# First two layers' last three tiles one by one, fewer products in the attention among slices, and small last groups in the de-slice

## The chip, the cores and the metric

One core of one Trainium2 chip runs one kernel launch. The metric is device time in microseconds (us); the median of several runs is the figure compared. The engines that appear below are TensorE (PE, with its weight loads as PEld), VectorE (DVE), ScalarE (ACT), GpSimd (POOL) and SyncE (SP), each with its own instruction queue; SP, ACT and POOL also issue DMAs (SPq, ACTq, POOLq).

## The reference

A graph of 6250 nodes with 256 features and 106,250 directed edges (loops among them) passes four blocks, each with a normalisation ahead of it and added to its input. Cut to what matters here:

```python
# block 1: two rounds of "sum over neighbours", each followed by an MLP (GIN)
h = (1 + eps1) * x + segment_sum(x[src], dst)          # layer 1
h = relu(h @ W1a + b1a); h = relu(h @ W1b + b1b)       # 256 -> 512 -> 512
h = (1 + eps2) * h + segment_sum(h[src], dst)          # layer 2
out = relu(h @ W2a + b2a) @ W2b + b2b                  # 512 -> 512 -> 256
# block 2: attention among 64 slices in each of 8 heads
fx = x @ W_fx + b_fx;  x_mid = x @ W_x + b_x
sw = softmax((x_mid @ W_slice + b_slice) / temp)       # node -> slice weights
token = einsum("nc,ng->gc", fx, sw) / (sw.sum(nodes) + 1e-5)   # per head
q, k, v = token @ W_q, token @ W_k, token @ W_v        # 64 x 64 each
o = softmax(q @ k.T * 64 ** -0.5) @ v
out = (sw @ o, heads side by side) @ W_out + b_out     # the de-slice
# block 3: a GCN layer (gather, sum, batch norm, relu) = layer 3
# block 4: a mixture of 8 experts, top 2, 256 -> 512 -> 256
```

The kernel applies W2a before the second sum over neighbours (the sum is linear), so that layer 1 writes h @ W2a as the table that layer 2 gathers from.

## The kernel before

**Tiles and chunks.** The nodes are cut into 49 tiles of 128 (tile 48 has 106). The sums over neighbours are made tile by tile: 831 chunks of 128 edges, 17 for a tile and 11 for tile 48. For each chunk POOL gathers 128 rows of a table in DRAM (L152); DVE builds a 128 x 128 matrix of zeros and ones that says which edge goes to which node; PE multiplies (L173, three bf16 products that together carry the fp32 value) and collects in PSUM. The class `Sums` does this, with a ring of gather buffers (10 deep in layer 1, 32 in layer 2). A table must be whole before the first gather of its layer: T2 (written at L698 in layer 1) for layer 2, T3 (written at L978 by ACT's DMA queue) for layer 3. Edges beyond the planned chunks are handled by `rest`, a loop that runs zero times on these inputs.

**Layers 1 and 2.** Tiles are grouped; when a group's sums are complete, a generator (`gin1` L652 to L700 for layer 1, `gin2` L784 to L865 for layer 2) gives the rest of its work in pieces. `staggered` (L354) puts these pieces between the chunks of the *next* group, so that PE works on one group's products while POOL gathers for the next. In `gin1` a group's pieces are the transposes (L349), W1a (L673), W1b (L681), and for each tile W2a (L688), the split into three bf16 parts (L691 to L697) and the writes of S2 and T2. In `gin2` they are the transposes of the sum (L804), W2b (L811), the normalisation, the transposes of the normalised tile (L349), the slice logits (L832), their softmax (L834 to L844), the token products (L852, added up in `tok`), and the transposed weights (L861), kept in SW for the de-slice. `begin` (L776) loads S2 for a group ahead of its sums.

`groups(4, 5)` in layer 1 gives fours, then [40-43], [44,45], [46,47], [48]. `groups(2)` in layer 2 gives pairs, then [46,47], [48]. `groups(4)` in the de-slice gives fours, then [44-47], [48].

**The attention core** (L870 to L952) runs once, after tile 48's token products: reciprocals of the slice sums (L889), the mean tokens and their transposes (L894 to L903), the token product with W_fx and the bias b_fx (L919, L920; for each of 8 heads two products of 128 rows and one of a single row), q and k (L926), v (L928), the logits (L930), their softmax (L934 to L940), the transposes (L941), o (L943), and W_out applied per head (L950), which gives M, 512 x 256. PE, DVE and ACT follow the order that the tile scheduler works out from the program; its PSUM buffers are those that layer 2 has freed.

**The de-slice** (L955 to L978) goes over the tiles once more: it reloads X1 and SW (three buffers of `swT`), multiplies SW with M (L968), adds, normalises for layer 3 (L329), splits into three bf16 parts (ACT L334, L337; DVE L335, L338), and writes T3. Layer 3 and the experts follow with an order written out by hand, which the change doesn't touch.

Of the kernel before, what the change touches and what calls it, by code (L numbers as in the profile page):

```python
# [9 lines left out]
F32 = mybir.dt.float32  # L10
BF16 = mybir.dt.bfloat16
I32 = mybir.dt.int32
AF = mybir.ActivationFunctionType
# [4 lines left out]
P = 128  # L18
# [3 lines left out]
def gin_transolver_gcn_moe(ctx: ExitStack, tc: tile.TileContext, a: dict, out: bass.AP):  # L22
# [38 lines left out]
    def groups(j, small=0):  # L61

        n = max(0, NT - small) // j * j
        out = [list(range(t, min(t + j, NT))) for t in range(0, n if small else NT, j)]
        while small and n < NT:
            m = 2 if NT - n > 2 else 1
            out.append(list(range(n, n + m)))
            n += m
        return out
# [281 lines left out]
            nc.scalar.activation(dest[:, k0:k0 + len(ks), :J * P],  # L351
                                 p[:, :len(ks) * J * P].rearrange("p (k n) -> p k n", k=len(ks)), AF.Copy)

    def staggered(gs, sums, finish, pieces):  # L354

        work = iter(())
        for ts in gs:
            nxt = finish(ts)
            for j, t in enumerate(ts):
                sums(t, lambda: next(work, None), (j + 1) * pieces // len(ts) - j * pieces // len(ts))  # L360
                next(nxt)
            for _ in work:
                pass
            work = nxt
        for _ in work:
            pass


# [386 lines left out]
    with tc.tile_pool(name="attn", bufs=1) as ap_:  # L755
# [3 lines left out]
        with tc.tile_pool(name="g2w", bufs=1) as wp:  # L759
# [5 lines left out]
            with tc.tile_pool(name="bn", bufs=1) as bnw, \  # L765
# [4 lines left out]

                needs = third_needs(bnw, ps)

                pairs = groups(2)
                s_of = {}

                def begin(ts):  # L776
                    s = w.tile([P, 2, HID], F32, name="s", bufs=3)
                    nc.sync.dma_start(s[:, :len(ts), :], tiles_of(S2, ts))
                    for j, t in enumerate(ts):
                        s_of[t] = s[:, j, :]  # L780

                begin(pairs[0])

                def gin2(ts):  # L784
                    J = len(ts)
                    if ts[0] in (4, 10):
                        next(needs, None)
                    xt = w.tile([P, 2, D], F32, name="xt")
                    if ts is not pairs[-1]:
                        begin(pairs[ts[0] // 2 + 1])  # L790
                    s = [s_of[t] for t in ts]
                    for j, t in enumerate(ts):
                        r = rows_of(t)
# [70 lines left out]
                            yield  # L864
                    nc.sync.dma_start(tiles_of(SW, ts), swT[:, :J, :])  # L865

                staggered(pairs, Sums(T2, msgs, 32, hots, ps, halves_added(lambda t: s_of[t], HID)), gin2, 11)


        res = ctx.enter_context(tc.tile_pool(name="res", bufs=1, side="right"))  # L870
# [2 lines left out]
        bw = back.enter_context(tc.tile_pool(name="desl", bufs=2))  # L873
        with tc.tile_pool(name="core", bufs=1) as w, \
                tc.tile_pool(name="core_ps", bufs=2, space=PSUM) as ps:
            Wfx = weights(w, a["L0_ffn_W_fx"], "Wfx")
            bfx = row(w, a["L0_ffn_b_fx"], H * C, "bfx")
            Wo = w.tile([C, H, D], F32, name="Wo")
            nc.sync.dma_start(Wo, a["L0_ffn_W_out"].rearrange("(h c) d -> c h d", c=C))
            wq = {}  # L880
            for n in ("W_q", "W_k", "W_v"):
                wq[n] = w.tile([C, C], F32, name=n)
                nc.sync.dma_start(wq[n], a["L0_ffn_" + n])

            def pst(name):
                return ps.tile([P, 512], F32, name=name, tag="mm")

            rec = w.tile([P, 2, KG], F32, name="rec")
            nc.vector.tensor_scalar(rec[:, 0, :], tok[:, :, D], 1e-5, None, op0=OP.add)  # L889
            nc.vector.reciprocal(rec[:, 0, :], rec[:, 0, :])  # L890
            nc.vector.tensor_mul(rec[:, 1, :], rec[:, 0, :], tok[:, :, D])
            prow = pst("prow")
            for m in range(KG):
                nc.vector.tensor_scalar(tok[:, m, :D], tok[:, m, :D], rec[:, 0, m:m + 1], None, op0=OP.mult)  # L894
                nc.tensor.transpose(prow[0:1, m * P:(m + 1) * P], rec[:, 1, m:m + 1], ident)
            nrow = w.tile([1, HG], F32, name="nrow")
            nc.vector.tensor_copy(nrow, prow[0:1, :HG])
            meanT = w.tile([P, KD, HG], F32, name="meanT")
            for k in range(KD):
                p = pst("pm")  # L900
                for m in range(KG):
                    nc.tensor.transpose(p[:, m * P:(m + 1) * P], tok[:, m, k * P:(k + 1) * P], ident)
                nc.vector.tensor_copy(meanT[:, k, :], p[:, :HG])  # L903

            def taken(p, name):
                t = w.tile([C, HG], F32, name=name)
                nc.vector.tensor_copy(t, p[:C, :HG])
                return t

            def per_head(name, f):  # L910
                p = pst("p" + name)
                for h in range(H):
                    s = slice(h * G, (h + 1) * G)
                    f(p[:C, s], s, h)
                return p

            def token(o, s, h):
                for k in range(KD):
                    nc.tensor.matmul(o, Wfx[:, k, s], meanT[:, k, s], start=(k == 0), stop=False)  # L919
                nc.tensor.matmul(o, bfx[:, s], nrow[:, s], start=False, stop=True)  # L920

            tokT = taken(per_head("tok", token), "tokT")
            qk = {}
            for n in ("W_q", "W_k"):
                p = pst("p" + n)
                nc.tensor.matmul(p[:C, :HG], wq[n], tokT, start=True, stop=True)  # L926
                qk[n] = taken(p, n + "T")
            v = taken(per_head("v", lambda o, s, h: nc.tensor.matmul(  # L928
                o, tokT[:, s], wq["W_v"], start=True, stop=True)), "v")
            p = per_head("l", lambda o, s, h: nc.tensor.matmul(  # L930
                o, qk["W_q"][:, s], qk["W_k"][:, s], start=True, stop=True))
            p3 = p[:C, :HG].rearrange("p (h g) -> p h g", g=G)
            mx = w.tile([C, 2, H], F32, name="mx")
            nc.vector.tensor_reduce(mx[:, 0, :], p3, axis=AX.X, op=OP.max)  # L934
            at = w.tile([C, H, G], F32, name="at")
            nc.vector.tensor_tensor(at, p3, mx[:, 0, :, None].to_broadcast([C, H, G]), op=OP.subtract)
            nc.scalar.activation(at, at, AF.Exp, scale=float(C) ** -0.5)
            nc.vector.tensor_reduce(mx[:, 1, :], at, axis=AX.X, op=OP.add)
            nc.vector.reciprocal(mx[:, 1, :], mx[:, 1, :])
            nc.vector.tensor_tensor(at, at, mx[:, 1, :, None].to_broadcast([C, H, G]), op=OP.mult)  # L940
            atT = taken(per_head("at", lambda o, s, h: nc.tensor.transpose(  # L941
                o, at[:, h, :], ident[:C, :C])), "atT")
            oT = taken(per_head("o", lambda o, s, h: nc.tensor.matmul(  # L943
                o, v[:, s], atT[:, s], start=True, stop=True)), "oT")

            for m in range(KG):
                p = pst("pM")
                for r in range(P // G):
                    h = m * (P // G) + r
                    nc.tensor.matmul(p[r * G:(r + 1) * G, :D], oT[:, h * G:(h + 1) * G], Wo[:, h, :],  # L950
                                     start=True, stop=True)
                nc.vector.tensor_copy(M[:, m, :], p[:, :D])  # L952


        with back, tc.tile_pool(name="desl_ps", bufs=2, space=PSUM) as ps:  # L955
            w = bw
            for ts in groups(4):
                J = len(ts)
                x1 = xr[:, ts[0]:ts[-1] + 1, :]
                nc.sync.dma_start(x1, block(X1, ts))  # L960
                swT = w.tile([P, 4, HG], F32, name="swT", bufs=3)
                nc.sync.dma_start(swT[:, :J, :], tiles_of(SW, ts))
                for j0 in range(0, J, 2):
                    js = range(j0, min(j0 + 2, J))
                    p = ps.tile([P, 2, D], F32, name="po", tag="mm", bufs=4)
                    for j in js:
                        for m in range(KG):
                            nc.tensor.matmul(p[:, j - j0, :], swT[:, j, m * P:(m + 1) * P], M[:, m, :],  # L968
                                             start=(m == 0), stop=(m == KG - 1))
                    nc.vector.tensor_add(x1[:, j0:js[-1] + 1, :], x1[:, j0:js[-1] + 1, :], p[:, :len(js), :])  # L970

                hs = w.tile([P, 4, D], F32, name="hs")
                layer_norm(w, x1, J, [hs[:, j, :] for j in range(J)], dinv[:, ts[0]:ts[-1] + 1],
                           ln3[:, :, ts[0]:ts[-1] + 1])
                hr = w.tile([P, 4, 3, D], BF16, name="hr")
                for _ in split(hr[:, :J], hs[:, :J, :], hs[:, :J, :], nc.vector.tensor_tensor):
                    pass
                nc.scalar.dma_start(block(T3, ts), hr[:, :J].rearrange("p j s f -> p j (s f)"))  # L978
# [406 lines left out]
```

## Time and profile before

| What | us |
|---|---|
| Six runs: median (lowest to highest) | 4011.18 (4002.73 to 4014.57) |
| Profiled execution: its own time / its span | 4004.99 / 4003.3 |
| First gather of layer 2 begins (from the span's start) | 1233.84 |
| Last gather of layer 2 issued | 2354.73 |
| Last token sum of layer 2 done, the core begins | 2396.60 |
| M done, the de-slice's products begin | 2427.09 |
| First gather of layer 3 begins | 2531.56 |

The span runs from the first to the last instruction. PE is busy for 74% of it and POOL for 65%, but the page's shares are means over stages with different limits; a stage's own window tells what limits it. A granted clock of 1.00 means that PE ran at full speed, 0.50 at half; a row's DMA share is the mean busy share of the 16 DMA engines. In a timeline row the bracket gives how long the engine stood idle before, and what ended that.

### The profile page before, as it was taken

What the parts mean: (1) busy time and instruction counts of PE and PEld (TensorE: products, weight loads), DVE (VectorE), ACT (ScalarE), POOL (GpSimd) and SP (SyncE); (2) the same over time, 40 slices, a digit from 0 to 9 for tenths busy, and PEclk for the clock granted to TensorE, in tenths of its full rate; (3) what the DMA queues carried; (4) which work ended last, traced back from release to release, by engine and by line L of the source; (5) the groups of instructions that cost most, each with busy time, mean ns of one, the idle gap of its engine ahead of it and who ended that gap; (6) DMA issues with size and microseconds to landing.
All of it is one profiled execution on the core that took longest, in us unless ns stands there. A gap on an engine that the chain in (4) does not pass through costs nothing. (4 is left out here: it accounts for less than half of the span.)

```text
span 4003.3 us, 44258 instructions
## 1 busy us (share of the span) xinstructions
PE 2976.3 (74%) x14455; PEld 1904.4 (48%) x14456; DVE 1525.9 (38%) x3910; ACT 783.3 (20%) x1474; POOL 2589.1 (65%) x2723
## 2 busy tenths in 40 slices
PE   2577787777886888888888879566777777777774
PEld 1344344444453444444444447344555566566654
DVE  7122222222322444444444446343334444433342
ACT  5011111111121111111111124111222222222221
POOL 3766677777764766676777730576766666666664
PEclk6588888898899999999999998667777887878887
DMA  6777777777777999999999966557777777778877
GB/s 197 241 265 257 271 247 252 242 251 224 238 239 267 323 323 318 319 327 328 325 333 326 321 233 224 154 167 251 261 261 251 239 250 244 257 262 302 287 262 231
DMA packets 352699, 1058.23 MB, mean 264 GB/s; under 512 B 60061, under 2 KB 147975, under 8 KB 337104
## 3 DMA queue, kind: packets, MB, share of 16 engines
q0 software_dynamic: 183024, 679.31, 52.2%
q1 hardware_dynamic: 162960, 366.42, 25.1%
q10 hardware_dynamic: 6480, 9.63, 0.7%
q8 instruction: 115, 1.88, 0.2%
q14 instruction: 120, 0.98, 0.1%
HBM read 881.24 MB, written 173.88 MB: 264 GB/s over the span
## 5 line engine op out<-in xcount | busy, mean ns | idle before, releaser
L152 POOL DMA_INDIRECT msg<-T,srcT x2493 | 2365.6, 949 | 1226.6 <-issue 615.8
L173 PE MATMUL pa<-msg,hot 128*128 128x257 bf16 (+2 forms) x7479 | 1514.3, 336 | 866.0 <-DMA msg<-T,srcT 819.8
L173 PEld LDWEIGHTS <-hot 128*128 128x128 bf16 x7479 | 782.0, 105 | 1533.7 <-issue 1147.8
L194 DVE SCALAR_TENSOR_TENSOR hot<-dstT,node 128x1152 bf16<-128x1152 f32 (+2 forms) x297 | 373.4, 1260 | 23.8 <-PE pa L173 23.8
L1208 PE MATMUL ph<-xdT,wb 128*128 128x128 f32 x1792 | 250.9, 290 | 45.3 <-DMA wb<-WB 24.9
L1208 PEld LDWEIGHTS ph<-xdT,wb 128*128 128x128 f32 x1792 | 226.8, 200 | 67.7 <-issue 21.6
L642 DVE TENSOR_TENSOR dinv<-dinv,pa 128x1 f32<-128x1 f32 x145 | 22.3, 154 | 591.9 <-PE pa L173 590.7
L1215 PE MATMUL py<-wb,hT 128*128 128x256 f32 x896 | 222.2, 392 | 0.1
L1210 ACT ACTIVATE hT<-ph,wb 128x128 f32<-128x128 f32 x448 | 163.8, 367 | 236.9 <-PE ph L1208 221.5
L681 PE MATMUL p<-h1T,W1b 128*128 128x512 f32 (+2 forms) x448 | 196.1, 586 | 0.0
L688 PE MATMUL p<-W2a,h2T 128*128 128x512 f32 x392 | 192.3, 637 | 0.0
L1215 PEld LDWEIGHTS py<-wb,hT 128*128 128x128 f32 x896 | 165.4, 195 | 22.5 <-ACT hT L1210 2.8
L998 DVE TENSOR_TENSOR s<-s,pa 64x256 f32<-64x256 f32 x96 | 40.2, 419 | 327.3 <-PE pa L173 325.2
L152 POOL DMA_INDIRECT g<-XD,place x98 | 95.6, 976 | 70.1 <-DMA XD<-yd 26.6
L351 ACT ACTIVATE sT<-pt 128x512 f32<-128x512 f32 (+1 forms) x25 | 14.7, 589 | 633.8 <-PE pt L349 633.8
L1111 POOL DMA_INDIRECT XD<-xn,place x98 | 97.4, 994 | 51.1 <-issue 18.0
L235 DVE TENSOR_TENSOR s<-s,pa 128x512 f32<-128x512 f32 x49 | 33.5, 683 | 251.1 <-PE pa L173 251.1
L236 DVE TENSOR_TENSOR s<-s,pa 64x512 f32<-64x512 f32 x48 | 33.2, 691 | 236.8 <-PE pa L173 236.8
L681 PEld LDWEIGHTS p<-h1T,W1b 128*128 128x128 f32 x448 | 86.6, 209 | 75.8 <-issue 73.2
L673 PE MATMUL p<-h0T,W1a 128*128 128x512 f32 (+2 forms) x224 | 120.4, 670 | 1.1 <-ACT h0T L351 0.5
L852 PE MATMUL ptok<-xn,sw 128*128 128x257 f32 (+1 forms) x392 | 103.0, 397 | 18.2 <-DVE sw L844 17.8
L688 PEld LDWEIGHTS p<-W2a,h2T 128*128 128x128 f32 x392 | 77.4, 208 | 81.4 <-issue 80.4
(303 smaller groups left out, 3069.8 us busy)
## 6 DMA issues: line engine op xcount, KB each, us to landing
wb<-WB SPq DMA_DIRECT2D x112, 1154.0 KB
XD<-zeros SPq DMA_DIRECT2D x102, 512.0 KB
msg<-T,srcT POOLq DMA_INDIRECT x2493
T<-tp SPq DMA_DIRECT2D x49, 384.0 KB
xd<-XD SPq DMA_DIRECT2D x112, 128.0 KB
XD<-yd SPq DMA_DIRECT2D x112, 128.0 KB
S<-s SPq DMA_DIRECT2D x49, 256.0 KB
s<-S SPq DMA_DIRECT2D x24, 512.0 KB
```

The lines of the kernel that those rows point to most:

```text
L152: return nc.gpsimd.indirect_dma_start(out=msg, out_offset=None, in_=table, in_offset=bass.IndirectOffsetOnAxis(ap=ix, axis=0))
L173: nc.tensor.matmul(pa[:, :n], hot, msg[:, s * F:s * F + n], start=(start and s == 2), stop=(stop and s == 1))
L194: nc.vector.scalar_tensor_tensor(hot[:, :n, :], dstT[:, c0:c0 + n, None].to_broadcast([P, n, P]), float(k * HALF), node2[:, k % 2, None, : ...
L673: nc.tensor.matmul(p[:, :T], W1a[:, k, m * P:(m + 1) * P], h0T[:, k, :T], start=(k == 0), stop=(k == KD - 1))
L681: nc.tensor.matmul(p[:, :T], W1b[:, k, m * P:(m + 1) * P], h1T[:, k, :T], start=(k == 0), stop=(k == KH - 1))
L688: nc.tensor.matmul(p, h2T[:, k, j * P:(j + 1) * P], W2a[:, k, :], start=(k == 0), stop=(k == KH - 1))
L852: nc.tensor.matmul(p[:, :D + 1], sws[j][:r, m * P:(m + 1) * P], xn[:r, j, :], start=(j == 0), stop=(j == J - 1))
L998: nc.vector.tensor_add(s3s[t][rows], s3s[t][rows], pa[rows, :D])
L1111: ins = nc.gpsimd.indirect_dma_start(out=XD[i], out_offset=bass.IndirectOffsetOnAxis(ap=place[:r, t, c:c + 1], axis=0), in_=xn[:r, j, :], ...
L1208: nc.tensor.matmul(p[:, :P], W1[:, k, m * P:(m + 1) * P], xdT[:, k, :P], start=(k == 0), stop=(k == KD - 1))
L1210: nc.scalar.activation(hT[:, m, :], p[:, :P], AF.Relu, bias=b1[:, m:m + 1])
L1215: nc.tensor.matmul(p[:, :D], hT[:, m, :], W2[:, m, :], start=(m == 0), stop=(m == KH - 1))
```

## The change

- `groups` gives pairs only while more than four tiles are left, so that `groups(4, 5)` ends in [44,45], [46], [47], [48]. Layer 2 uses `groups(2, 3)`, which ends in ..., [44,45], [46], [47], [48], and the de-slice `groups(4, 5)`.
- `staggered` gets `aside`: in layer 2 only 5 of tile 47's 11 pieces go between tile 48's chunks; then two pieces of 48, and then 47's other pieces and 48's in turn. `begin` loads S2 two groups ahead.
- In the core, two products of weights alone are formed first: kq from W_q and W_k, and vo from W_v and W_out for each head (three 64 x 64 transposes, one 64 x 64 product, four 64 x 512 products). The logits then come from tokT and one product kq by tokT; v is formed with vo (64 x 256 for each head) and M from the attention and v, so that q, the product o and its copy go. b_fx is added by one product of 8 rows with a mask `of_head` instead of eight of one row. PSUM tiles have four buffers instead of two, and some copies move from DVE to ACT.

```diff
@@ groups
-            m = 2 if NT - n > 2 else 1
+            m = 2 if NT - n > 4 else 1
@@ staggered
-    def staggered(gs, sums, finish, pieces):
+    def staggered(gs, sums, finish, pieces, aside=False):
         work = iter(())
         for ts in gs:
             nxt = finish(ts)
+            n = pieces // 2 if aside and ts is gs[-1] else pieces
             for j, t in enumerate(ts):
-                sums(t, lambda: next(work, None), (j + 1) * pieces // len(ts) - j * pieces // len(ts))
+                sums(t, lambda: next(work, None), (j + 1) * n // len(ts) - j * n // len(ts))
                 next(nxt)
+            if n < pieces:
+                break
             for _ in work:
                 pass
             work = nxt
+        for _ in range(2):
+            next(nxt, None)
         for _ in work:
+            next(nxt, None)
+        for _ in nxt:
             pass
@@ layer 2
-                pairs = groups(2)
+                pairs = groups(2, 3)
...
                 begin(pairs[0])
+                begin(pairs[1])
...
-                    if ts is not pairs[-1]:
-                        begin(pairs[ts[0] // 2 + 1])
+                    if ts not in pairs[-2:]:
+                        begin(pairs[pairs.index(ts) + 2])
...
-                staggered(pairs, Sums(...), gin2, 11)
+                staggered(pairs, Sums(...), gin2, 11, True)
@@ core
             def pst(name):
-                return ps.tile([P, 512], F32, name=name, tag="mm")
+                return ps.tile([P, 512], F32, name=name, tag="mm", bufs=4)
...
+            of_head = w.tile([H, H, G], F32, name="of_head")
+            nc.vector.memset(of_head, 1.0)
+            for op, base in ((OP.is_ge, 0), (OP.is_gt, 1)):
+                nc.gpsimd.affine_select(out=of_head, in_=of_head, ...)
+            p = pst("pwT")
+            for i in range(3):
+                nc.tensor.transpose(p[:C, i * C:(i + 1) * C], wq[:, i, :], ident[:C, :C])
+            wT = w.tile([C, 3, C], F32, name="wT")
+            nc.scalar.activation(wT, p[:C, :3 * C].rearrange("p (i c) -> p i c", i=3), AF.Copy)
+            p = pst("pkq")
+            nc.tensor.matmul(p[:C, :C], wT[:, 1, :], wT[:, 0, :], start=True, stop=True)
+            kq = w.tile([C, C], F32, name="kq")
+            nc.scalar.activation(kq, p[:C, :C], AF.Copy)
+            vo = w.tile([C, H, D], F32, name="vo")
+            for h in range(0, H, 2):
+                p = pst("pvo")
+                nc.tensor.matmul(p[:C, :2 * D], wT[:, 2, :], Wo[:, h:h + 2, :], start=True, stop=True)
+                nc.scalar.activation(vo[:, h:h + 2, :], p[:C, :2 * D].rearrange("p (h d) -> p h d", h=2), AF.Copy)
...
-                for k in range(KD):
-                    nc.tensor.matmul(o, Wfx[:, k, s], meanT[:, k, s], start=(k == 0), stop=False)
-                nc.tensor.matmul(o, bfx[:, s], nrow[:, s], start=False, stop=True)
+            p = pst("ptok")
+            nc.tensor.matmul(p[:C, :HG], bfx, nrow, start=True, stop=False)
+            for h in range(H):
+                o = slice(h * G, (h + 1) * G)
+                for k in range(KD):
+                    nc.tensor.matmul(p[:C, o], Wfx[:, k, o], meanT[:, k, o], start=False,
+                                     stop=(h == H - 1 and k == KD - 1))
...
-            for n in ("W_q", "W_k"):
-                p = pst("p" + n)
-                nc.tensor.matmul(p[:C, :HG], wq[n], tokT, start=True, stop=True)
-                qk[n] = taken(p, n + "T")
-            v = taken(per_head("v", lambda o, s, h: nc.tensor.matmul(
-                o, tokT[:, s], wq["W_v"], start=True, stop=True)), "v")
-            p = per_head("l", lambda o, s, h: nc.tensor.matmul(
-                o, qk["W_q"][:, s], qk["W_k"][:, s], start=True, stop=True))
+            p = pst("pk")
+            nc.tensor.matmul(p[:C, :HG], kq, tokT, start=True, stop=True)
+            kT = taken(p, "kT")
+            p = pst("pl")
+            for h in range(H):
+                o = slice(h * G, (h + 1) * G)
+                nc.tensor.matmul(p[:C, o], tokT[:, o], kT[:, o], start=True, stop=True)
...
+            v = w.tile([C, H, D], F32, name="v")
+            for h in range(0, H, 2):
+                p = pst("pv")
+                for i in range(2):
+                    nc.tensor.matmul(p[:C, i * D:(i + 1) * D], tokT[:, (h + i) * G:(h + i + 1) * G], vo[:, h + i, :],
+                                     start=True, stop=True)
+                nc.scalar.activation(v[:, h:h + 2, :], p[:C, :2 * D].rearrange("p (h d) -> p h d", h=2), AF.Copy)
...
-            oT = taken(per_head("o", lambda o, s, h: nc.tensor.matmul(
-                o, v[:, s], atT[:, s], start=True, stop=True)), "oT")
...
-                    nc.tensor.matmul(p[r * G:(r + 1) * G, :D], oT[:, h * G:(h + 1) * G], Wo[:, h, :],
+                    nc.tensor.matmul(p[r * G:(r + 1) * G, :D], atT[:, h * G:(h + 1) * G], v[:, h, :],
@@ de-slice
-            for ts in groups(4):
+            for ts in groups(4, 5):
```

## The prediction

> **What bounds the kernel now.** I read, in this order, the page's table of groups, then PE's waits and the windows around the four stretches that the diff touches, then the timeline of each. The page first (engine sums, and the two groups that fill the layers; the last columns are busy time, mean of one, and idle time before with what ended it):
>
> ```profile
> PE 2976.3 (74%) x14455; PEld 1904.4 (48%) x14456; DVE 1525.9 (38%) x3910; ACT 783.3 (20%) x1474; POOL 2589.1 (65%) x2723
> L152 POOL DMA_INDIRECT msg<-T,srcT x2493 | 2365.6, 949 | 1226.6 <-issue 615.8
> L173 PE MATMUL pa<-msg,hot 128*128 128x257 bf16 (+2 forms) x7479 | 1514.3, 336 | 866.0 <-DMA msg<-T,srcT 819.8
> ```
>
> The three layers are paced by POOL's gathers. No gather of a layer can start before the previous layer's table is whole, so between layers POOL stands still, and those two gaps are what this change can shorten:
>
> ```profile
> 1233.84 0.94 POOL L152 DMA_INDIRECT msg<-T,srcT  x1 [39.30 <-issue]
> 2531.56 0.94 POOL L152 DMA_INDIRECT msg<-T,srcT  x1 [175.89 <-issue]
> ```
>
> The bracket is POOL's idle time. Gap 1 (39.30 us) is the end of layer 1. Gap 2 (175.89 us) is the end of layer 2, the attention core, and the de-slice. In the windows (length, then busy time and instructions of PE, PEld, DVE, ACT, POOL; granted clock; DMA) I see four regimes:
>
> ```profile
> 1149.36:1212.98 63.62, 56.46 (x272) 40.10 (x270) 15.01 (x29) 13.55 (x26) 33.09 (x35) 0.92 0.62 203
> 1212.98:1233.84 20.86, 10.08 (x59) 7.20 (x58) 7.83 (x14) 6.44 (x15) 0.00 (x1) 0.89 0.71 204
> 2359.00:2396.60 37.60, 22.28 (x69) 13.64 (x68) 16.79 (x34) 9.32 (x14) 0.00 (x0) 0.82 0.42 137
> 2404.00:2428.00 24.00, 17.24 (x94) 11.08 (x93) 8.72 (x15) 1.91 (x2) 0.00 (x0) 0.50 0.79 254
> 2432.00:2513.70 81.70, 81.70 (x379) 71.62 (x377) 64.70 (x169) 46.10 (x76) 0.00 (x0) 1.00 0.60 206
> PE pa L173 <- DMA msg<-T,srcT: 7.1, 6, 2.1
> ```
>
> Row 1 is tiles 46 to 48 of layer 1 on PE, row 2 tile 48's own multilayer part, row 3 the same end in layer 2, row 4 most of the core at half clock, row 5 the de-slice, PE without a hole. The last line is PE's wait list in row 1's window: 7.1 us in six waits, all on gathers.
>
> **Layer 1's end.** Moved: the products of [44,45] into tile 46's sums, of 46 into 47's, of 47 into 48's; before, [44,45] was spread over 46 and 47, and [46,47] all fell on 48, where PE was busy 20.88 of the 20.88 us from 1192.10 to 1212.98. A single tile costs 2.58 (L673) + 3.79 (L681) + 3.60 (L688) + 0.44 (L349) = 10.4 us on PE; the pair's rows give 4.96, 3.62 + 1.89 + 1.89 = 7.40, and 7.20, so two singles cost 0.4 us more than a pair. A chunk is 20.7 us / 45 = 0.46 us on PE (the 135 L173 matmuls of row 1's window); POOL issued 35 gathers in the 44.24 us to 1193.60, 1.26 us each. So tile 46 asks PE for about 20 + 17 x 0.46 = 28 us against 17 x 1.26 = 21.5 us of gathers, and PE falls 6 us behind; tile 47 asks for 10.4 + 7.8 = 18.2 against 21.5, which the lag covers; tile 48 asks 10.4 + 5.1 = 15.5 against 13.9. No gather should be waited for: -7.1 + 0.4 = -6.7. The ring of ten buffers passes part of the lag back to POOL (it waited 6.2 us for L173 in this window already), so I take **-5**. Ends: all waits return, +0.4; all go and PE works at full clock (56.46 x 0.08 = 4.5 more), -11. Tile 48's own chain (row 2) and its last table write keep their instructions.
>
> **Layer 2's end.** Tile 48 alone began late because PE's order put the pair's softmax first:
>
> ```profile
> 2369.59 5.24 PE L852 MATMUL ptok<-xn,sw 128*128 128x257 f32 x16 [4.86 <-DVE sw L844]
> 2375.95 0.92 PE L804 MATMUL ph<-ident,s 128*128 128x128 f32 x4 [0.25 <-ACT swT L862]
> 2376.86 1.99 PE L811 MATMUL p<-W2b,h4T 128*128 128x256 f32 x8
> 2392.35 3.79 PE L852 MATMUL ptok<-xn,sw 106*128 106x257 f32 x8 [5.89 <-DVE sw L844]
> ```
>
> Its last chunk was done near 2360.0; 20.65 us from 2375.95 bring 2396.6. In the changed order, after chunk 8 of 48's eleven come 46's four token products, its transposes, 47's first transposes and W2b: 1.7 + 0.5 + 0.9 + 1.0 us of PE that put the last chunk some 2.5 us later (2362.5). Then tile 47's normalisation (3.4 us on DVE and ACT from W2b at 2360.8) gives its transposes at 2364.2, its logits by 2366.5, its softmax (three DVE passes of 0.7, table load 1.28, exp 0.6, then 0.7 + 0.2 + 0.7) by 2372. Tile 48's transposes slip into that, but its W2b product stands behind the first two token products of 47: about 2373, 3.9 us before 2376.86. Behind it 47's other token products, their four 0.42 us DVE adds and its transposes share the engines with 48's chain: I give back half and take **-2**. Ends: full side by side (48 from 2361 plus 20.65, plus some 7 us of 47's DVE work) is 2389, -7; one after the other with the late chunk and a half clock, +3. What queues behind PE's wait for the softmax is 48's W2b, and behind that the core. SP issues one more set of loads for each group added; each S2 load (L778) now stands two groups ahead, and before nothing on SP that the chain waits for: 0; a load met late would cost its own 2 us.
>
> **The core.** The rows of before (two passes per fp32 product):
>
> ```profile
> 2407.35 1.97 PE L926 MATMUL pW_q<-tokT,W_q 64*64 64x512 f32 x2 [0.78 <-DVE tokT L907]
> 2409.11 1.91 PE L926 MATMUL pW_k<-tokT,W_k 64*64 64x512 f32 x2
> 2418.34 1.03 PE L941 MATMUL pat<-ident,at 64*64 64x64 f32 x8 [3.90 <-DVE at L940]
> 2420.15 1.96 PE L943 MATMUL po<-atT,v 64*64 64x64 f32 x16 [0.78 <-DVE atT L907]
> 2422.88 3.68 PE L950 MATMUL pM<-Wo,oT 64*64 64x256 f32 x16 [0.77 <-DVE oT L907]
> ```
>
> Added, ahead of everything (PE's order has them before the first normaliser transpose, and their PSUM is free only when layer 2's is): three 64x64 transposes (3/8 of 1.03 = 0.4), one ACT copy with its waits (0.6), one small product (0.2), four products 64x512. These cost 1.75 each cold (2407.35 to 2409.11) and, the clock having been 0.93 from 2396 to 2404, perhaps 0.9: 3.6 to 7. Less what PE waited anyhow: +4.4 to +7.5, I take +5.0, as the clock there was high. Removed: the 16 single-row bias passes of the token product's 48 (L920, eight pairs at 0.25 to 0.41 from start to start, some 2.6 in all), against one new 512-column bias product (0.9 to 1.75): -0.9 to -1.7, I take -1.5. W_q and W_k become one product, W_v's leaves this place: 7.12 us from 2407.35 to the logits' end become 1.97 + 0.78 + 1.91 = 4.66, -2.5. The eight new 64x256 products cost what pM's cost, 3.68, and lie in PE's 3.90 us wait for the softmax: 0, and the full 3.68 if that cover goes. po and its copy go: 2422.88 - 2420.15 = -2.7. Copies moved to ACT lie beside DVE's, and ACT was busy 1.91 of 24 us there: 0. The head mask (one DVE fill after the last chunk's sum, two POOL instructions) lies in POOL's 175.89 us gap and some 35 us ahead of its reader: 0; late, it would hold the bias product and all after it. Sum -1.7; I take **-1.5**. Ends: all cold, +2.3, rounded to +3; all at full clock, halving the 20 us from tokT on, -7.5.
>
> The clock row: 0.50 from 2404 to 2428 though PE was busy 17.24 of 24 us, and in 2408 to 2412 4.00 of 4.00. The Trainium skill (TensorE: Matmul & The Clock Gate, Part 1) says that some 3.4 us of sustained work bring the full clock; by it the fuller PE of the new core would warm up and the sum for the core would be -7.5. The row shows a busy PE that stays at half, so I follow the row.
>
> **The de-slice's end.** Now [44,45], [46], [47], [48]. The last table write before:
>
> ```profile
> 2524.89 0.92 ACTq L978 DMA_DIRECT2D T<-hr  x2
> ```
>
> PE ended near 2513.74. Smaller groups let normalising and splitting begin earlier, but ACT runs them one after another, each table write waiting for DVE in ACT's own queue: following their order with the rows' durations per tile (L329 0.5, L334 and L337 0.3, L335 and L338 0.3) I reach 2524.8 for tile 48's write, and its slice weights come about 1 us later to PE, as their buffer frees after [44,45]. The write is a single tile, and one issue rather than two (0.5): **-0.5**, ends -4 and +3.
>
> Sum: -5 - 2 - 1.5 - 0.5 = -9 us. The profiled run took 4004.99 (span 4003.3, 1.7 around it): it would be 3996. It lies 6.2 below the median of the six runs, 4011.18 (4002.73 to 4014.57), so against that median: **4002 us**.
>
> **Rivals.**
> - *Everything lands*: all waits of layer 1 gone (-6.7), layer 2 side by side (-7), core warm (-7.5), de-slice -2: -23, about 3988. For it: PE idle 15 us of 37.6 in row 3. Against: the half clock in row 4.
> - *The chains only move*: layer 1's waits come back elsewhere (-2), layer 2 at 0, weight products cold on the path (+2), de-slice 0: no change, 4009 to 4013. For it: tile 48's chain is untouched and all that is moved must run before it or beside it.
> - *The clock falls in layer 1's end* (the slower side): single tiles mean 128-column products with an ACT step between. If the granted clock over row 1's work fell from 0.92 to 0.70, 56.46 us would be 74.2, +18; with the -5 gone and the other -4 kept, +14: 4025. It decides below a clock of about 0.75. Against: tile 48's own products, of that form, had 0.89.
>
> **How the numbers follow.** Forecast 45% (3996 to 4008), everything lands 22%, chains move 20%, clock 13%. What this kernel's measurement can tell from no change is about 0.2%, 8 us: faster is below 4003.2, slower above 4019.2. Faster: 22% and some 27 of the forecast's 45, 49%; slower: the clock, 13%, and 1% of scatter; the rest 37%. Range: the four pairs of ends combined as root of squares give about -10 and +9 around 4002; toward the other cases and the scatter of medians, 3990 to 4018. The forecast's own: 3996 to 4008.
>
> **What would show it.** Right: PE's waits for layer 1's gathers in tiles 46 to 48 near zero and gap 1 near 34 us; 48's W2b product in layer 2 3 to 4 us sooner; between layer 2's last transposes and the normaliser row some 5 us of weight products, but the logits-to-M stretch 2.7 shorter; gap 2 near 172. Wrong: waits still there, 0.50 during the weight products, or the last table write more than 13 us after the de-slice's last product.

## The result and the profile after

The changed kernel took 3999.65 us (median of 21 runs, 3989.33 to 4012.51) where the kernel before took 4009.06 (42 runs, 3998.53 to 4025.76): ratio 0.9975, 95% interval 0.9967 to 0.9983, or about 9.4 us less. Its profiled execution took 4002.86 us, span 4001.2; the profiled execution of before took 4004.99. So the two profiled executions differ by 2.1 us only: the one of before lies 4.1 below its median, the one after 3.2 above. What follows tells which stretches changed; it can't account for all of the 9.4.

POOL's two gaps in the changed kernel, from its timeline (the bracket is the idle time before):

```profile
1226.86 0.94 POOL L152 DMA_INDIRECT msg<-T,srcT  x1 [28.42 <-issue]
2530.36 0.94 POOL L152 DMA_INDIRECT msg<-T,srcT  x1 [168.37 <-issue]
```

They were 39.30 and 175.89. But a gap begins when POOL issues its last gather, and that moved too: in layer 1 from 1193.60 to 1197.50. Layer 2's first gather came 7.0 us earlier, not 10.9. Layer 3's came 1.2 us earlier, so 5.8 of the 7.0 were given back between them.

The windows of the changed kernel that answer to those of before (length, busy time and instructions of PE, PEld, DVE, ACT, POOL; granted clock; DMA share; GB/s), and PE's wait list in the first:

```profile
1146.73:1205.92 59.19, 53.33 (x320) 38.89 (x318) 15.21 (x29) 15.55 (x35) 33.07 (x35) 1.00 0.67 226
1205.92:1226.86 20.94, 11.35 (x59) 8.65 (x58) 7.52 (x14) 6.30 (x15) 0.00 (x0) 0.81 0.60 183
2392.50:2401.40 8.90, 7.75 (x13) 2.15 (x13) 1.22 (x5) 2.91 (x6) 0.00 (x0) 0.50 0.62 191
2401.40:2427.50 26.10, 23.28 (x109) 13.85 (x108) 7.19 (x12) 4.82 (x9) 0.00 (x0) 0.57 0.60 193
PE pa L173 <- DMA msg<-T,srcT: 5.6, 6, 1.7
```

The same work in layer 1, from the end of [40-43]'s last W2a to tile 48's own transposes, took 64.6 us before (1149.36 to 1213.95) and 59.9 after (1146.73 to 1206.58). The clock there was 1.00, no longer 0.92, and the waits for gathers are still 5.6 us. Rows 3 and 4 are the core: the first is new time in which PE forms products of weights, at half clock.

In layer 2's end and the core, from PE's timeline of the changed kernel:

```profile
2371.87 2.08 PE L861 MATMUL ptok<-xn,sw 128*128 128x257 f32 x4 [5.67 <-DVE sw L853]
2373.74 3.04 PE L820 MATMUL p<-W2b,h4T 128*128 128x256 f32 x8
2387.84 3.77 PE L861 MATMUL ptok<-xn,sw 106*128 106x257 f32 x8 [4.64 <-DVE sw L853]
2393.19 0.53 PE L914 MATMUL pwT<-ident,wq 64*64 64x64 f32 x3 [0.74 <-ACT swT L871]
2394.45 7.03 PE L924 MATMUL pvo<-Wo,wT 64*64 64x512 f32 x8
2401.41 1.87 PE L933 MATMUL prow<-ident,rec 128*8 128x128 f32 x8
...
2414.53 7.03 PE L972 MATMUL pv<-vo,tokT 64*64 64x256 f32 x16
2421.49 1.06 PE L980 MATMUL pat<-ident,at 64*64 64x64 f32 x8
2423.41 3.68 PE L986 MATMUL pM<-v,atT 64*64 64x256 f32 x16 [0.87 <-DVE atT L890]
```

Tile 48's W2b product comes right behind two of 47's token products, as PE's order has it. From 2393.19 to 2401.41 PE forms weights while everything else waits. The values (L972) take 7.03 us; DVE had the softmax ready at 2419.24, and the transposes that read it begin at 2421.49, when the values end. In the de-slice the last product ended at 2513.95 and the table's last write was issued at 2527.05, 13.1 us later; before, the last two writes were issued 11.1 and 11.6 us after the last product.

The stretches of the two traces, in us:

| Stretch | before | after |
|---|---|---|
| Layer 1, same work to tile 48's transposes | 64.6 | 59.9 |
| Layer 2, first to last gather issued | 1120.9 | 1124.4 |
| Last gather issued to last chunk done on PE | 5.3 | 7.9 |
| Last chunk to tile 48's last transposes | 36.8 | 33.3 |
| Last transposes to the normaliser's product (prow) | 0.7 | 9.0 |
| prow to the de-slice's first product | 29.6 | 26.2 |
| De-slice, first to last product | 86.7 | 86.4 |
| Last product to layer 3's first gather | 17.8 | 16.4 |

### The profile page after: what moved, and what is told of

The parts are those of the page before. It is cut to its first block, busy times and chain, and to the rows that moved or that the text cites. A ratio compares the mean times of both kernels' runs of the same rounds, so it can differ in the third digit from the quotient of the medians.

```text
span 4001.2 us, 44408 instructions
## 1 busy us (share of the span) xinstructions
PE 2977.4 (74%) x14488; PEld 1898.6 (47%) x14489; DVE 1527.6 (38%) x3926; ACT 795.9 (20%) x1508; POOL 2590.4 (65%) x2725
## 5 line engine op out<-in xcount | busy, mean ns | idle before, releaser
L1147 POOL DMA_INDIRECT XD<-xn,place x98 | 97.7, 997 | 50.8 <-issue 16.8
L820 PE MATMUL p<-W2b,h4T 128*128 128x256 f32 x392 | 114.8, 390 | 0.0
```

Source lines behind the costliest of these rows:

```text
L820: nc.tensor.matmul(p[:, j, :], h4T[:, k, j * P:(j + 1) * P], W2b[:, k, :], start=(k == 0), stop=(k == KH - 1))
L1147: ins = nc.gpsimd.indirect_dma_start(out=XD[i], out_offset=bass.IndirectOffsetOnAxis(ap=place[:r, t, c:c + 1], axis=0), in_=xn[:r, j, :], ...
```

## The experiments

They ran on three other chips, called the second, third and fourth here, on which every kernel took 10 to 12% longer. So a ratio is compared only with the ratios of its own chip (each against the kernel before there), a stretch with gathers only with the same stretch there, and only stretches without gathers from chip to chip. Those repeat: from layer 2's last transposes to the de-slice's first product ("the core stretch") the old core took 30.2 us on the first chip and 29.9 to 31.2 on the others. Each kernel has one trace on each chip. Layer 3 and the experts, which no part touches, took 1662.6 to 1669.2 us in the four traces of the second chip, so a difference of a few microseconds between whole traces shows nothing.

**Second chip: each part alone** (before: 4471.16 us).

Layer 1's groups alone: `m = 2 if NT - n > 4 else 1`, with the rest as before.

> The kernel before with only layer 1's last groups changed ([44,45], [46], [47], [48]). Theory A (the sizes of the prediction, PE's waits for gathers go): 5 us less than before, with the first gather of layer 2 some 5 to 7 us earlier. Theory B (the part of the two traces is the whole effect and the others only shift it): 7 us less here, and the sum of the four single parts is near the 9.4 us of the whole. Rival: tile 48's own chain sets the end and nothing is gained: within 2 us of before.

Measured: 0.9971 (0.9951 to 0.9990). From the first gather of the kernel to the last write of layer 1's table: 1244.0 us, against 1251.5, 1257.1 and 1255.0 in the other three kernels on this chip, which leave layer 1 alone. So the part gains, 7 to 13 us there, and the rival falls. The end of layer 1, the stretch of the first line of the table above, took 64.4 us against 73.8, 74.1 and 72.8. PE was busy for 54.7 us of it against 57.0, 57.9 and 59.5 (clock 0.97 against 0.91, 0.91 and 0.88) and idle for 9.7 against 16.8, 16.1 and 13.4: on this chip the larger share of the gain is in PE's idle time, not in the clock.

Layer 2's end alone:

```diff
-                pairs = groups(2)
+                pairs = groups(2, 3, 4)
-                staggered(pairs, Sums(...), gin2, 11)
+                staggered(pairs, Sums(...), gin2, 11, True)
```

> The kernel before with only layer 2's end changed (single tiles, the last two side by side). Theory A: 2 us less, tile 48's W2b product 3 to 4 us nearer to the last gather. Theory B, from the two traces (last gather to the end of the last transposes 42.1 before, 41.2 after): 1 us less. Rival: 47 and 48 hold each other up, 0 to 3 us more.

Measured: 0.9952 (0.9929 to 0.9975, seven runs). From the last chunk to the last transposes 31.3 us, against 36.0, 37.0 and 36.8 in the other three. Tile 48's W2b product began 12.9 us after the last chunk instead of 17.0 to 17.9. The stretch is shorter on the first chip too (33.3 against 36.8); the ratio is larger than that stretch can give (5 of 4471 us are 0.1%), and where the rest is from isn't settled.

The core alone:

> The kernel before with only the attention core changed. Theory A (prediction): 1.5 us less. Theory B, from the two traces (8.3 us more from the last transposes to the normaliser's product, 3.4 less from there to the de-slice): 5 us more than before. From the end of layer 2's transposes to the first de-slice product: 28.7 by A, 35 by B.

Measured: 0.9994 (0.9971 to 1.0017), no difference to be told. Last transposes to the first de-slice product: 32.2 us against 30.8, 29.9 and 30.0. Not 28.7, so theory A falls; less than 35, because the clock rose before the token product in this trace (2.08 us for its 32 passes, 3.51 in the trace of the changed kernel).

The de-slice's groups alone:

> The kernel before with only the de-slice's last groups changed. Theory A: 0.5 us less. Theory B, from the two traces (17.8 us from the last product to the first gather of layer 3 before, 16.4 after): 1.4 us less. Rival: the slice weights that come late for tiles 47 and 48 eat it, 0 to 2 us more.

Measured: 0.9984 (0.9965 to 1.0003). Last product to the first gather of layer 3: 16.6 us, against 17.1, 17.6 and 17.8. That is 0.5 to 1.2 less, between the theories' 0.5 and 1.4. The last write came later, 13.1 us after the last product against 11.6, and the first gather sooner after it, 3.5 us against 5.6 to 6.3. The rival falls.

**Third chip: the core taken apart** (before: 4465.74 us).

> The changed kernel itself, on the chip of the next three, so that they can be compared with it. The four parts measured singly had ratios 0.9971, 0.9952, 0.9994 and 0.9984, on a chip on which every kernel took some 11% longer. If the parts add up and scale with the chip, the whole is near 0.990 there, and 0.9975 on a chip like the first.

Measured: 1.0000 (0.9978 to 1.0022), with the trace's core stretch at 35.1 us as on the first chip. The product of the four ratios is 0.990. With some 0.002 on each, the product is uncertain by 0.004 and the whole by 0.002, so the two differ by about twice what these runs can tell. Either the parts don't add up on these chips, or two of the four came out too good; that stays open.

Products of weights early: as generators between layer 1's chunks, kept in DRAM.

```diff
+                if ts[0] >= 8:
+                    next(early, None)
                 h0T = w.tile([P, KD, 512], F32, name="h0T")
...
+            vo = w.tile([C, H, D], F32, name="vo")
+            nc.sync.dma_start(vo, VO)
```

> The changed kernel with the eight products of weights formed in layer 1 (one to five at a time, from tile 8 on), kept in DRAM and loaded for the core as the weights were. Theory A (they stand on the path: 8.2 us from the transposes of the weights to the normaliser's product in the profile of the changed kernel): 7 to 8 us less than the changed kernel, the normaliser's product within 1 us of layer 2's last transposes. Rival (they fill a wait that is there anyway): within 2 us.

Measured: 0.9965 (0.9943 to 0.9987); median 4451.04 against 4464.45 for the changed kernel on this chip. PE's timeline of this kernel:

```profile
2651.78 1.04 PE L948 MATMUL prow<-ident,rec 128*8 128x128 f32 x8 [0.74 <-ACT swT L902]
...
2660.45 6.35 PE L987 MATMUL pv<-vo,tokT 64*64 64x256 f32 x16
```

The normaliser's product follows the transposes after 0.74 us, so the products stood on the path and filled no wait. The core stretch is 21.8 us, 13.3 less, more than the 8.2 removed, because what follows ran at a higher clock (prow 1.04 us instead of 1.87, the token product 2.08 instead of 3.51). Layer 1 took 1253.8 us from its first gather to its table's last write, against 1248.2 for the changed kernel: about 5 us seem to be paid there. The medians differ by 13.4 us where 7 to 8 were expected.

The values in both halves of PSUM:

```diff
-                    nc.tensor.matmul(p[:C, i * D:(i + 1) * D], tokT[:, (h + i) * G:(h + i + 1) * G], vo[:, h + i, :],
+                        nc.tensor.matmul(p[r * C:(r + 1) * C, j * D:(j + 1) * D], tokT[:, h * G:(h + 1) * G], vo[:, h, :],
                                          start=True, stop=True)
```

> The changed kernel with the value products of odd heads written to PSUM partitions 64 to 127 and those of even heads to 0 to 63, as the products for M are; the attention's transposes become products with the identity, so that they can be written likewise. Theory A (two 64-column products in different halves of PSUM run beside each other, those in one half one after the other: 3.68 us for M's, 7.03 for the values): the values take 3.6 us, the attention's transposes begin when the softmax is done, 2 to 3 us less than the changed kernel. Rival (the values take 7 us for another reason): 7.0 us and no gain.

Measured: 0.9984 (0.9959 to 1.0009). PE's timeline of this kernel:

```profile
2667.25 3.62 PE L974 MATMUL pv<-vo,tokT 64*64 64x256 f32 x15
2672.03 1.12 PE L983 MATMUL pat<-ident,at 64*64 64x64 f32 x16 [1.17 <-DVE at L979]
2673.77 3.68 PE L991 MATMUL pM<-v,atT 64*64 64x256 f32 x16 [0.62 <-DVE atT L986]
```

The first row has 15 of the 16 passes; with the one that began 0.17 us before it they took 3.8 us instead of 7.03, and the transposes now wait for DVE's softmax: theory A. The clock isn't the cause: it was granted at 0.50 in the first row's 3.62 us as it was in the 7.03, and M's products next to them took the same 3.68 us in both kernels. The core stretch was 27.9 us. That is more than the values can give: the weights' products took 5.32 us here and the token product 2.08, at a higher clock than in the traces with 35.1.

Both edits together:

> The two edits together: by theory A of each, 10 to 11 us less than the changed kernel, and the stretch from layer 2's last transposes to the de-slice's first product 24 us where it was 35.1 in the profile of the changed kernel and 30.2 in the one before.

Measured: 0.9961 (0.9939 to 0.9983), 4447.03 us, the lowest median on this chip, 17.4 us under the changed kernel. Core stretch 21.7 us, 24 expected; layer 1 again longer, 1255.1. With the early products alone the core stretch was 21.8, so in these two traces the halves add nothing to it: the normaliser's product and the mean tokens' transposes ran slower again (1.88 and 1.90 us against 1.04 and 1.09), which took back what the values saved.

**Fourth chip: the gap between the layers, and the old core** (before: 4436.71 us).

> The changed kernel once more, beside the next three. Theory A (the change's gain lies in the ends of the layers, where PE works without POOL, and doesn't depend on the chip): 0.9975 where kernels take some 4000 us; on a chip where they take some 4460, 0.997 to 0.999, as 9 us of 4460 are 0.2%. Theory B (on the slower chip the gathers' late landing hides the ends' gain): 0.999 to 1.001 there.

Measured: 0.9990 (0.9967 to 1.0012). With 1.0000 on the chip before, the gain on these chips is smaller than what the runs can tell, or hidden; neither theory is decided. The traces of the slower chips show what could hide it: from the last gather of layer 2 to its last chunk on PE took 31.8 to 44.2 us there, against 5.3 and 7.9 on the first chip. In the changed kernel's trace here the four 64x512 products took 5.06 us and the core stretch 30.0, in the same kernel that took 7.03 and 35.1 twice.

Products of weights after tile 48's chain of layer 1 (with a dependency that keeps ACT's copies behind the last split):

```diff
             staggered(groups(4, 5), sums1, gin1, 1 + 2 * KH + 4)
+            for _ in early:
+                pass
```

> Both edits to the core (halves of PSUM; products of weights off the path), but the products of weights are formed after tile 48's own chain of layer 1, where PE waits for the first gather of layer 2 (14 us idle in the profile of the changed kernel), and not among layer 1's chunks. Theory A (among the chunks they cost what PE takes for them, since PE is what layer 1's end waits for; in the gap they cost nothing): the stretch from layer 2's last transposes to the de-slice's first product 21.7 us, the last gather of layer 1 to the first of layer 2 as in the changed kernel, 13 us less than it in all. Rival (they delay the table's last write or layer 2's first chunk): the gap 3 us or more longer.

Measured: 0.9989 (0.9970 to 1.0007), 4429.75 us against 4431.68 for the changed kernel. The core stretch is 19.3 us, but the timeline at the end of layer 1 shows the rival:

```profile
1326.22 0.33 SPq L737 DMA_DIRECT2D T<-tp  x1
1326.93 7.03 PE L685 MATMUL pvo<-Wo,wT 64*64 64x512 f32 x8
1334.00 0.59 ACT L686 ACTIVATE vo<-pvo 64x512 f32<-64x512 f32 x1 [1.12 <-PE pvo L685]
1334.95 2.35 SPq L819 DMA_DIRECT2D s<-S  x3
1341.93 0.94 POOL L154 DMA_INDIRECT msg<-T,srcT  x1 [42.94 <-DMA s<-S]
```

From the table's last write to the first gather 15.7 us instead of 3.5. SP's loads and DVE go on only after ACT's last copy, though they need nothing from it: the loop `rest`, which runs zero times between the layers, is a point that the engines pass together. In this trace SP's queue stands at the loop's own line (L248) for 2.4 us until PE arrives and 0.3 us more until ACT does. POOL began 7 us later still; the DRAM write of vo, issued at 1335.83, lies in between, but what POOL waited for there was not tried.

With the de-slice's small groups written from SP's queue:

```diff
-                nc.scalar.dma_start(block(T3, ts), hr[:, :J].rearrange("p j s f -> p j (s f)"))
+                (nc.scalar if J == 4 else nc.sync).dma_start(block(T3, ts), hr[:, :J].rearrange("p j s f -> p j (s f)"))
```

> As the kernel before it in this call, with the de-slice's small groups written to the table from SP's queue instead of ACT's. Theory A (ACT waits in its own queue for DVE before each of these writes: five holes of 0.65 to 0.88 us in the profile of the changed kernel): the last write 10 to 11 us after the de-slice's last product where it was 13.1, 2 to 3 us less. Rival (the chain is DVE's and ACT's in turn, whoever issues the write): 0 to 1 us.

Measured: 0.9982 (0.9963 to 1.0001). Last product to the first gather of layer 3: 15.4 us against 16.0 in the kernel without this edit. The rival: 0.6 us, as the steps of DVE and ACT follow one another whoever issues the write.

The changed kernel with the old core:

> The changed kernel with the attention core of the kernel before. Theory A (the new core as it stands costs 4.9 us, 35.1 against 30.2 from layer 2's last transposes to the first de-slice product): 5 us less than the changed kernel. Theory B (the new core pays, as the prediction had it): 1.5 us more than the changed kernel.

Measured: 0.9992 (0.9971 to 1.0013); median 4427.27, 4.4 under the changed kernel, but inside each other's intervals. The core stretch was 31.2 us against 30.0 for the changed kernel on the same chip (its high-clock trace). By the traces of all chips the new core's stretch is 30.0 to 35.1 and the old one's 29.9 to 31.2: it doesn't pay, and whether it costs depends on the clock in that execution.

## Why the prediction came out

The forecast was -9 us (4002); measured was -9.4 (3999.65). The total was right, but not every step, and the terms as the traces have them don't sum to it. All three things that the prediction named as showing it wrong came: waits for gathers still there (5.6 us), a clock of 0.50 during the weight products, and the last table write more than 13 us after the last product (13.1).

- **Layer 1, -5 forecast.** The same work took 4.7 us less, and the part alone gained. The size holds; the reason given holds by half. PE's waits for gathers were to vanish, as the lag from tile 46 would cover tile 47. They went from 7.1 to 5.6 us and moved into 47 and 48. In this pair of traces the larger share is PE's busy time, 56.46 to 53.33 us, with the clock at 1.00 instead of 0.92: the bound that was named only as the far end. On the second chip it is PE's idle time (9.7 us against 13.4 to 16.8), so there the prediction's reason holds better; which of the two it is in most executions of the first chip, one trace of each kernel can't show. Of the 7.0 us by which layer 2 begins earlier, 2.6 were there before the first changed instruction.
- **Layer 2, -2.** The last chunk was to come 2.5 us later and did by 2.6 (5.3 to 7.9 after the last gather); 48's W2b product was placed at 2373 and stands at 2373.74, but that is luck: the last gather came 3.5 us earlier in this trace. Counted from the last gather the product began after 22.5 us instead of 22.1, so it came no sooner, where 3 to 4 us were forecast. Counted from the last chunk it came 2.2 us sooner, which the late chunk took back, and what follows it took 1.3 less. Net -0.9.
- **The core, -1.5.** This step failed: +4.9, beyond its end of +3. Three terms were mis-sized. For the weights, the prediction took "+5.0, as the clock there was high"; they cost 8.2 us, at 0.50 throughout. For the values, "cost what pM's cost, 3.68": they cost 7.03, because pM's row writes two halves of PSUM and theirs one half, so they ran past the softmax by 2.2 us. The early and the halved kernels show both. A row of before had the right price: the prediction took 1.75 us for two passes of 512 columns in one half (L926) and used it for the weights; for the values, four times as many columns, it gives 7.0. Of the 6.7 us to be saved from prow to the de-slice's first product 3.4 came (29.6 to 26.2). One product in place of W_q's and W_k's, with W_v's gone from there, gave 3.6 up to the logits' end where 2.5 were forecast, at a clock of 0.84 instead of 0.50. From prow to that product nothing was saved (9.8 us before, 9.9 after), where the bias was to give 1.5, at a clock of 0.56 instead of 0.80. From the logits' end to the de-slice nothing was saved either (12.7 and 12.8), as the longer values took back what the product o had cost.
- **The de-slice, -0.5.** -1.7: 0.3 in the products and 1.4 behind them. The last write came 13.1 us after the last product instead of 11.6, later than forecast, but the next gather began 3.3 us after it instead of 6.3. The kernel with only this part shows the same (3.5 against 5.6 to 6.3); that a single tile's smaller write is the reason is likely and not shown.

From the traces: -4.7 - 0.9 + 4.9 - 1.7 = -2.4 (-2.5 before rounding). The two profiled executions differ by 2.1, as the stretches in which nothing was changed come to +0.4: -2.6 ahead of layer 1's end, +0.4 from there to the first gather of layer 2, +3.5 over layer 2's gathers, -0.9 from layer 3 on. The medians differ by 7 more than the changed stretches. The stretches full of gathers vary by such amounts from one execution to the next (on the second chip layer 2's took 1222.7, 1225.6 and 1228.1 us in three kernels that leave layer 2 alone), so a single trace of each kernel can't show where the 7 are. So the core's error of 6.4 us was made good by something not located: the total is no proof of the steps.

Of the rivals, "everything lands" failed in layer 1's waits and the core's clock, and "the clock falls" turned round: in layer 1's end it rose. "The chains only move" has the core's half clock, though not the values' cost, and may be what the other chips showed (1.0000 and 0.9990).

## What to carry to other kernels

Before products are folded to shorten a chain, see where the scheduler puts the folding: work that needs only weights stood ahead of the chain here for 8 us, and moving it away gave 13 us in the medians, where the folding by itself gave nothing that the runs can tell. A free-looking gap is only free if no point at which all engines meet lies behind it. Price a new product by a row with the same output partitions, not only the same shape, and don't trust the sum of one pair of traces beyond what executions of one kernel differ by.

## What the hardware showed unexpectedly

Products of 64 output rows written to different halves of PSUM ran beside each other: 16 passes of 64x256 took 3.8 us in two halves and 7.03 in one, with operands on the same 64 partitions and a granted clock of 0.50 for both.

PE's clock stayed at 0.50 in a stretch where PE was busy 7.75 of 8.90 us, and on from there: from 2393.19 to 2410.18 in the profile of the changed kernel PE was busy 16.53 of 16.99 us, at 0.50 throughout. In another execution of the same kernel the clock was high when the weights' products began, and after a low stretch it rose earlier. The rows of the changed kernel on two other chips, the same two stretches (weights, then prow to the first de-slice product):

```profile
2651.80:2660.70 8.90, 7.74 (x13) 2.15 (x13) 1.22 (x5) 2.91 (x6) 0.00 (x0) 0.50 0.60 186
2660.70:2686.80 26.10, 23.29 (x109) 13.88 (x108) 7.19 (x12) 4.82 (x9) 0.00 (x0) 0.57 0.60 194
```

```profile
2633.50:2640.20 6.70, 5.51 (x13) 1.49 (x13) 1.23 (x6) 2.91 (x6) 0.00 (x0) 0.75 0.51 175
2640.20:2663.40 23.20, 20.36 (x109) 11.84 (x108) 7.19 (x12) 4.83 (x9) 0.00 (x0) 0.65 0.74 239
```

The same instructions, 35.0 and 29.9 us. The Trainium skill (TensorE: Matmul & The Clock Gate, Part 1) says that the deciding window runs freely, so that a run's phase shifts the clock's rise; the two pairs of rows, 0.50 and 0.57 against 0.75 and 0.65, are in keeping with that, but no run here shows the phase. It says too that some 3.4 us of sustained work bring the full clock; the 16.99 us at 0.50 do not agree, and the measurement decides. Why these products leave the clock low no run here shows.
